# A second buffer for transposed blocks, paid for with shared places, in a graph attention and slice attention layer on one Trainium2 core

## The chip, the cores and the metric

The kernel runs on one core of one Trainium2 chip. The metric is the device time of one launch in microseconds (us). Before the change the median of three runs is 2681.41 us (2673.46 to 2681.55). The profiled execution has a span of 2673.3 us.

A core has a matrix engine (TensorE, PE in the profile, with its weight loads as PEld), a vector engine (VectorE, DVE), a scalar engine for functions such as Exp (ScalarE, ACT), GpSimd (POOL), and SyncE (SP), whose queue issues the DMA transfers here. All of them run at the same time, each through its own list of instructions in order, and wait for one another by semaphores.

## What is computed

The input x has 32 batches of 512 rows (nodes) and 256 features. Each batch passes two residual blocks. In short form:

```python
# block 1: graph attention, twice
o0 = relu(ln(x) @ mlp1_w + b1)                  # 512 x 512
h  = o0 @ W_fc                                  # unmasked attention
p  = softmax(leaky_relu(f1[i] + f2[j]), axis=j) # f1, f2: h times two vectors
o1 = elu(elu(p @ h)) + o0
o2 = relu(o1 @ mlp2_w + b2)                     # 512 x 256
h2 = o2 @ W_hand                                # attention masked by adj
p2 = softmax(where(adj > 0, leaky_relu(f1[i] + f2[j]), -9e15), axis=j)
x  = x + relu(elu(elu(p2 @ h2)) + o2)

# block 2: slice attention with 8 heads, 64 slices of 64 channels
xn = ln(x)
w  = softmax((xn @ W_x) @ W_slice / temperature)    # 512 x (8 x 64)
tokens = (w.T @ (xn @ W_fx)) / sum(w)               # per head
out_slice = softmax(q @ k.T / 8) @ v                # q, k, v from tokens
out = x + (w @ out_slice) @ W_out + b_out
```

Everything is in float32. The batches are independent of one another, and the kernel keeps up to four of them in progress.

## The kernel before

The kernel is written batch by batch and step by step, but isn't emitted in that order. A recorder takes down every operation with the tiles that it reads and writes; then a list scheduler with its own model of costs plays the program through, and the operations are emitted in the order of their modelled starts. TURNS gives each step of a batch a point in time that serves as its priority; HEAD and TAIL shift the steps of the first and the last three batches.

```python
TURNS = {
    "load": -145.1, "norm1": -102.2, "mlp1": 176.5, "h": 203.5, "factors": 206.6, "p": 209.3,
    "pv": 219.9, "o1": 240.0, "mlp2": 243.4, "h2": 273.9, "e": 274.6, "p2": 274.6,
    "pv2": 305.6, "norm2": 314.1, "w": 376.2, "sums": 378.3, "s1T": 396.3, "tokens": 446.2,
    "att": 472.7, "vo": 472.7, "gg": 472.7, "out": 483.8,
}
PERIOD, SPARE = 92.2, 0.00
```

A tile belongs to a tag, and a tag has so many places (bufs, one by default) in on-chip memory. A tile can only be begun when a place of its tag is free, and the scheduler also keeps a queue for each tag: whose turn it is to take the next place. For most tags that queue runs through all batches in order; for tags that begin with "stage" each batch has a queue of its own.

```python
class _Log:
    def __init__(self, ap, age):            # age: number of the batch
        ...
        self.queue = self.tag, age if self.psum or self.tag.startswith("stage") else 0
```

Large transposes of inner batches don't run on PE. VectorE transposes 32x32 blocks into a stage tile, four DMAs write the stage to a scratch tensor in DRAM, and a fifth reads it back with the blocks in their new places (the first and the last batch use PE transposes instead):

```python
def flip(src, dst):
    nc.vector.transpose(dst, src.rearrange("p (c i) -> p c i", i=Q))      # Q = 32

def gather(what, stage, dst):
    blocks, width = stage.shape[1:]
    scr = dram.tile([blocks, Q, P // Q, width], F32, name="scr", tag=f"scr_{what}", bufs=2)
    for a in range(P // Q):
        nc.sync.dma_start(scr[:, :, a, :].rearrange("c r j -> r c j"), stage[ts(a, Q), :, :])
    nc.sync.dma_start(dst, scr.rearrange("(k c) r a j -> (c r) k (a j)", c=P // Q))
```

Three of these stages, u_stage, e_stage and w_stage, are 8 KiB per partition and share the tag "stage" with one place. The smaller ones (for xn, o2, xn2 and s1) share another tag, "stage4", also with one place.

```python
# step pv: unmasked attention, for each block i of 128 rows
u, m = row("u"), row("m")                    # tags u and m, two places each
elu_elu([...], m, u)
flip(u, stage[:, :, ts(i, Q)])               # u_stage
# step o1
gather("u", stage, o1T)                      # then o1T += o0T on VectorE, four instructions

# step mlp2
o2T = new("o2T", [P, KD, N])
...  # 8 matmuls from o1T, two ScalarE instructions write o2T
# step e: masked attention, for each block i
...  # three VectorE instructions and one Exp on tile e
flip(e, stage[:, :, ts(i, Q)])               # e_stage
# step p2
gather("e", stage, pT)
...  # o2T is also transposed for the residual, through o2_stage
# step pv2
u, m = row("u2", (P, 2, D), "u"), row("m2", (P, 2, D), "m")
elu_elu(parts, m, u)

# step norm2
raw = new("xn2_raw", [P, KD, N], tag="raw4")
transpose_features("xn2", b, xn, raw, True)  # flips into xn2_stage, gather into raw
...  # two ScalarE copies from raw to xn2T
# step w
wt = softmax of (xn2T @ weff) by blocks of rows
flip(wt, stage_w[:, :, ts(t, Q)])            # w_stage
# step sums: s1 = w.T @ xn, gather("w", ...), four ScalarE copies into wT
# steps s1T, tokens
# steps att, vo
sc = new("sc2", [P, NP, G])
...  # softmax of the slice attention in sc, PE transposes of sc into pt
attT = new("attT", [P, NP, G])
nc.scalar.copy(attT, pt)
# steps gg, out
```

Of the kernel before, what the change touches and what calls it, by code (L numbers as in the profile page):

```python
# [13 lines left out]
ENGINES = ("tensor", "vector", "scalar", "gpsimd", "sync")  # L14

TURNS = {
    "load": -145.1, "norm1": -102.2, "mlp1": 176.5, "h": 203.5, "factors": 206.6, "p": 209.3,
    "pv": 219.9, "o1": 240.0, "mlp2": 243.4, "h2": 273.9, "e": 274.6, "p2": 274.6,
    "pv2": 305.6, "norm2": 314.1, "w": 376.2, "sums": 378.3, "s1T": 396.3, "tokens": 446.2,
    "att": 472.7, "vo": 472.7, "gg": 472.7, "out": 483.8,  # L20
}
PERIOD, SPARE = 92.2, 0.00

HEAD = (
    (-8, -8, 49, -10, -8, 25, 0, -39, -4, 6, -2, -2, -40, -2, -2, -2, -2, -2, 3, -8, 1, -20),
    (8, 2, 25, 1, 1, 0, 8, 8, 1, 1, -7, 0, 2, 2, 2, 2, 2, 2, 2, -5, 9, 2),
    (0, -1, -1, 0, 0, -22, 0, 12, 0, 1, 0, 0, 0, 0, 0, 0, 11, 0, 0, 0, -3, 0),
)
TAIL = (
    (0, 0, 53, 0, 0, 0, 0, 4, 0, 0, -6, 2, 0, 0, 0, 0, 2, 0, 3, 3, -5, 4),  # L30
    (0, 0, 17, 1, -2, -27, 0, -2, -4, -38, 0, 23, 1, -6, -2, 9, 2, 6, -2, -2, -2, -2),
    (-85, 1, 1, 1, 1, 16, 20, 22, 19, 19, 19, 7, 14, -7, 9, 9, -7, 0, -7, 0, -16, -30),
)


# [4 lines left out]
P = 128  # L40
# [4 lines left out]
class Recorder:  # L45
# [10 lines left out]
    def __init__(self, nc):  # L56
        self.nc, self.ops, self.logs, self.age, self.step = nc, [], {}, -1, ""
        self.joint = False
        for engine in ENGINES:
            setattr(self, engine, _Recording(self, engine))  # L60
# [215 lines left out]
class _Log:  # L276


    def __init__(self, ap, age):
        tensor = ap.tensor  # L280
        self.name, self.tag, self.bufs = tensor.name, tensor.tag, tensor.tag_meta.bufs
        self.psum = ap.space == bass.MemoryType.PSUM

        self.queue = self.tag, age if self.psum or self.tag.startswith("stage") else 0
        self.entries = []


# [22 lines left out]
def adj_ffn_kernel(  # L310
# [26 lines left out]
    B, N, D = x.shape  # L337
    HID = mlp1_w.shape[1]
    HH = HID // 2
    NT = N // P  # L340
    KD = D // P
    KH = HID // P
    HEADS = temperature.shape[1]
    G = W_slice.shape[1]
    C = W_slice.shape[0]
    INNER = HEADS * C
    NP = INNER // P
# [11 lines left out]
    def new(name, shape, bufs=1, tag=None, dtype=F32):  # L359
        return sbuf.tile(list(shape), dtype, name=name, tag=tag or name, bufs=bufs)  # L360

    def mm_tile(shape):
        return psum.tile(shape, F32, tag="mm", name="mm", bufs=5)
# [8 lines left out]
    Q = 32  # L372
# [5 lines left out]
    def by_dma(what, b):  # L378

        return what in FLIPPED and b not in EDGES  # L380
# [35 lines left out]
    def load_x(b):  # L416
# [14 lines left out]
        out=ident, in_=ident, compare_op=OP.not_equal, fill=1.0, base=0,  # L431
# [160 lines left out]
    for p in range(NP):  # L592
        pv = mm_tile([P, D])
# [49 lines left out]
    def front(b):  # L643
# [21 lines left out]
        h = new("h", [P, NT, 2, HH + 1])  # L665
# [49 lines left out]
        nc.step = "pv"  # L715
        o1T = new("o1T", [P, KH, N])
        if by_dma("u", b):
            stage = new("u_stage", [P, HID // Q, P], tag="stage")
        for i in range(NT):
            pms = [mm_tile([P, HH + 1]), mm_tile([P, HH])]  # L720
            for s, pm in enumerate(pms):
# [21 lines left out]
        if by_dma("u", b):  # L743
            gather("u", stage, o1T)
            for m in range(KH):
                o1 = o1T[:, m, :].rearrange("p (t a i) -> p t a i", t=NT, i=Q)
# [3 lines left out]
    def middle(b, o1T):  # L750

        nc.step = "mlp2"
        o2T = new("o2T", [P, KD, N])
        for m in range(KD):
            pm = mm_tile([P, N])
            for k in range(KH):
                nc.tensor.matmul(
                    pm.rearrange("p (a t i) -> p a t i", t=NT, i=Q), w2[:, k, ts(m)],
                    swapped(o1T[:, k, :]), start=(k == 0), stop=(k == KH - 1),
                )  # L760
            nc.scalar.activation(o2T[:, m, :], pm, AF.Relu, bias=b2[:, m : m + 1])
        nc.step = "h2"
        h = new("h2", [P, NT, D + 2])
        for t in range(NT):
            pm = mm_tile([P, D + 2])
            for k in range(KD):
                nc.tensor.matmul(
                    pm, o2T[:, k, ts(t)], wh[:, k, :], start=(k == 0), stop=(k == KD - 1)
                )
            nc.scalar.copy(h[:, t, :], pm)  # L770
        f2b = tr_tile([P, N])
        for j in range(NT):
            nc.tensor.transpose(f2b[:, ts(j)], h[:, j, D + 1 : D + 2].to_broadcast([P, P]), ident)
        if not by_dma("e", b):
            pt, f2b = f2b, new("f2b", [P, N], tag="acb")
            nc.scalar.copy(f2b, pt)
        nc.step = "e"
        pT = new("p2T", [P, NT, N])
        if by_dma("e", b):
            stage = new("e_stage", [P, N // Q, P], tag="stage")  # L780
        nmax = small("nmax", [P, NT])
        for i in range(NT):
            e = new("e", [P, N], bufs=2)
            nc.vector.scalar_tensor_tensor(
                e, f2b, h[:, i, D : D + 1], mbias[:, i, :], op0=OP.add, op1=OP.add
            )
            nc.vector.scalar_tensor_tensor(e, e, ALPHA, e, op0=OP.mult, op1=OP.max)
            nc.vector.tensor_reduce(
                nmax[:, i : i + 1], e, axis=AX.X, op=OP.max, negate=True
            )  # L790
            nc.scalar.activation(e, e, AF.Exp, bias=nmax[:, i : i + 1])
            if by_dma("e", b):
                flip(e, stage[:, :, ts(i, Q)])
                continue
            pt = tr_tile([P, NT, P])
            for j in range(NT):
                nc.tensor.transpose(pt[:, j, :], e[:, ts(j)], ident)
            nc.scalar.copy(
                pT.rearrange("p j (t a i) -> p j t a i", t=NT, i=Q)[:, :, :, i, :],
                pt.rearrange("p j (t i) -> p j t i", i=Q),  # L800
            )
        nc.step = "p2"
        if by_dma("e", b):
            gather("e", stage, pT)

        nc.vector.memset(h[:, :, D], 1.0)

        r2 = new("r2", [P, NT, D])
        stage = new("o2_stage", [P, N // Q, KD * Q], tag="stage4")
        for k in range(KD):  # L810
            nc.vector.transpose(
                stage[:, :, ts(k, Q)].rearrange("p (t a) i -> p t a i", t=NT),
                swapped(o2T[:, k, :]),
            )
        gather("o2", stage, r2)

        x1 = new("x1", [P, NT, D], bufs=2)
        nc.sync.dma_start(x1, x[b].rearrange("(p t) d -> p t d", p=P))
        nc.step = "pv2"
        for i2 in range(NT // 2):  # L820
            parts = []
            for s in range(2):
                i = 2 * i2 + s
                pm = mm_tile([P, D + 1])
                for j in range(NT):
                    nc.tensor.matmul(
                        pm, pT[:, j, ts(i)], h[:, j, : D + 1], start=(j == 0), stop=(j == NT - 1)
                    )
                rd = small("rd2", [P, 1])
                nc.vector.reciprocal(rd, pm[:, D : D + 1])  # L830
                parts.append((pm[:, :D], rd, s))
            u, m = row("u2", (P, 2, D), "u"), row("m2", (P, 2, D), "m")
            elu_elu(parts, m, u)
            for s in range(2):
                u3 = u[:, s, :].rearrange("p (k a i) -> p k a i", k=KD, i=Q)
                r3 = r2[:, 2 * i2 + s, :].rearrange("p (a k i) -> p k a i", k=KD, i=Q)
                nc.vector.tensor_tensor(u3, u3, r3, op=OP.add)
            nc.vector.scalar_tensor_tensor(
                x1[:, ts(i2, 2), :], u, 0.0, x1[:, ts(i2, 2), :], op0=OP.max, op1=OP.add
            )  # L840
        return x1

    def back(b, x1):
# [4 lines left out]
        layernorm(x1, xn, "ln2")  # L848
        xnT = new("xn2T", [P, KD, N])
        if by_dma("xn2", b):  # L850
            raw = new("xn2_raw", [P, KD, N], tag="raw4")
            transpose_features("xn2", b, xn, raw, True)
            for k in range(KD):
                nc.scalar.copy(
                    xnT[:, k, :].rearrange("p (t a i) -> p t a i", t=NT, i=Q), swapped(raw[:, k, :])
                )
        else:
            transpose_features("xn2", b, xn, xnT, False)

        nc.step = "w"  # L860
        w = new("w", [P, NT, INNER])
        wT = new("wT", [P, NP, N])
        if by_dma("w", b):
            stage_w = new("w_stage", [P, INNER // Q, P], tag="stage")
        for t in range(NT):
            pm = mm_tile([P, INNER])
            for k in range(KD):
# [29 lines left out]
        if by_dma("s1", b):  # L897
            stage = new("s1_stage", [P, D // Q, P], tag="stage4")
# [20 lines left out]
        if by_dma("w", b):  # L919
            raw = new("w_raw", [P, NP, N], tag="w")  # L920
# [6 lines left out]
        s1T = med("s1T", (P, KD, INNER))  # L927
# [74 lines left out]
        pt = tr_tile([P, NP, G])  # L1002
        for q in range(NP // 2):
            nc.tensor.transpose(pt[:, ts(q, 2), :], sc[:, ts(q, 2), :], ident)
        attT = new("attT", [P, NP, G])
        nc.scalar.copy(attT, pt)
        pa = mm_tile([P, NP, G])
        halves(pa, tokbd, attT)
# [2 lines left out]
        gg = med("gg")  # L1011
        for p2 in range(NP // 2):
            pg = mm_tile([P, 2, D])
            for s in range(2):
                p = 2 * p2 + s
# [87 lines left out]
```

## Time and profile before

| what | value |
|---|---|
| median of three runs | 2681.41 us (2673.46 to 2681.55) |
| span of the profiled execution | 2673.3 us |
| instructions | 35248 |
| DMA traffic | 375.40 MB, mean 140 GB/s |
| ACT busy | 1093.4 us (41%) |
| POOL busy | 111.8 us (4%) |

The page gives for every engine its busy time and its share of the span; then the span in 40 equal slices with the busy share of each in tenths (9 is 90% or more), and the clock that PE was granted, in tenths of full speed. As every operation is emitted by the same helper line of the kernel (L273), groups are told apart by the tiles they write and read: "mm<-h,pT" is a matmul into a tile mm from h and pT. "mm" is the tag of most matmul outputs, "tr" that of PE transposes. One float32 matmul shows as two records. In a list of waits, "PE mm <- DVE o1T" is time in which PE could not start a matmul because VectorE had not yet written o1T. In a timeline a bracket after a line gives the idle time of the engine just before it and what ended it.

### The profile page before, as it was taken

The page shows a single profiled execution, that of the slowest core. Times are in us where ns is not written, and L with a number is a line of the kernel's source. Part 1 is how long each engine was busy: PE and PEld are TensorE (multiplying, and loading weights), DVE is VectorE, ACT ScalarE, POOL GpSimd, SP SyncE. Part 2 cuts the span into 40 slices and gives each one's busy share as a digit, 9 for nine tenths or more (in the row PEclk, how much of TensorE's full clock was granted, in tenths as well). Part 3 has the DMA queues.
Part 4 walks back from the last instruction along what each step waited for, and adds up shares of the span by engine and source line. Part 5 has one row for each costly group of instructions (what it writes and reads, how often), then busy time and mean ns, then how long its engine had stood idle before and what let it go on. Part 6 is the DMA issues. An engine that isn't in the chain of part 4 may idle for free.

```text
span 2673.3 us, 35248 instructions
## 1 busy us (share of the span) xinstructions
PE 2608.7 (98%) x12477; PEld 1929.1 (72%) x12477; DVE 2081.2 (78%) x5161; ACT 1093.4 (41%) x2009; POOL 111.8 (4%) x171
## 2 busy tenths in 40 slices
PE   7999999999999999999999999999999999999997
PEld 5776667777777777777777777776777767777775
DVE  6577778877778877779877788777788777888785
ACT  3443344433444433444434444334444334444341
POOL 1000000000000000000000000000000000000000
PEclk9999999999999999999999999999999999999998
DMA  5125455554455454556554555544564545554440
GB/s 162 52 67 148 122 156 166 152 156 132 137 166 166 137 161 116 147 168 165 148 141 128 157 166 148 154 127 139 168 172 134 154 122 150 166 158 142 127 119 23
DMA packets 465657, 375.40 MB, mean 140 GB/s; under 512 B 86597, under 2 KB 382665, under 8 KB 465481
## 3 DMA queue, kind: packets, MB, share of 16 engines
q1 hardware_dynamic: 463896, 372.10, 49.6%
q8 instruction: 99, 1.62, 0.2%
q10 hardware_dynamic: 1584, 1.05, 0.1%
q14 instruction: 78, 0.63, 0.1%
HBM read 197.96 MB, written 175.11 MB: 140 GB/s over the span
## 4 chain that ended last, share of the span: by engine, by line
PE 45%; DVE 29%; DMA 16%; issue 3%; SPq 3%; POOL 2%; ACT 1%; DVEq 0%; ACTq 0%
PE mm L273 43%; DMA xt<-in_x_dram 5%; DVE u L273 4%; DVE e L273 3%; DMA o1T<-scr 3%; DMA scr<-e_stage 3%; SPq L273 3%; PE tr L273 2%; DVE w L273 2%; POOL ln_rstd L273 2%; DVE e_stage L273 2%; DVE w_stage L273 2%; DMA scr<-u_stage 2%; DVE m L273 1%; DVE u_stage L273 1%
## 5 line engine op out<-in xcount | busy, mean ns | idle before, releaser
L273 PE MATMUL mm<-wfc,o0T 128*128 128x257 f32 x2048 | 479.3, 381 | 0.0
L273 PE MATMUL mm<-h,pT 128*128 128x257 f32 (+1 forms) x2048 | 468.1, 380 | 4.2 <-DVE pT L273 4.2
L273 PEld LDWEIGHTS mm<-wfc,o0T 128*128 128x128 f32 x2048 | 381.9, 189 | 82.2 <-issue 24.8
L273 PEld LDWEIGHTS mm<-h,pT 128*128 128x128 f32 x2048 | 385.2, 190 | 64.3 <-DVE pT L273 6.7
L273 ACT COPY h<-mm 128x257 f32<-128x257 f32 (+1 forms) x384 | 142.9, 372 | 302.2 <-PE mm L273 295.8
L273 PE MATMUL mm<-xn,w 128*128 128x257 f32 x1024 | 255.1, 383 | 4.0 <-ACT w L273 3.3
L273 PE MATMUL mm<-xnT,w 128*128 128x512 f32 x512 | 240.4, 600 | 10.8 <-DMA xnT<-scr 7.3
L273 PE MATMUL mm<-gg,wT 128*128 128x256 f32 x1024 | 245.3, 379 | 0.0
L273 PE MATMUL mm<-h,p2T 128*128 128x257 f32 x1024 | 244.9, 380 | 0.3 <-ACT o0T L273 0.3
L273 PE MATMUL mm<-o1T,w 128*128 128x512 f32 x512 | 227.4, 596 | 13.4 <-DVE o1T L273 10.8
L273 PE MATMUL mm<-weff,xn2T 128*128 128x512 f32 x512 | 231.7, 595 | 0.0
L273 PEld LDWEIGHTS mm<-h,p2T 128*128 128x128 f32 x1024 | 191.4, 190 | 31.3 <-ACT o0T L273 0.7
L273 PEld LDWEIGHTS mm<-xn,w 128*128 128x128 f32 x1024 | 187.8, 191 | 35.0 <-issue 8.9
L273 PEld LDWEIGHTS mm<-gg,wT 128*128 128x128 f32 x1024 | 191.7, 190 | 28.6 <-issue 1.0
L273 PEld LDWEIGHTS mm<-o1T,w 128*128 128x128 f32 x512 | 94.8, 190 | 131.0 <-issue 94.5
L273 DVE STREAM_TRANSPOSE o_stage<-o2T 128x512 f32<-128x512 f32 x64 | 45.5, 710 | 163.6 <-ACT o2T L273 163.6
L273 ACT ACTIVATE e<-e,nmax 128x512 f32<-128x512 f32 x128 | 92.4, 722 | 186.0 <-DVE nmax L273 184.5
L273 DVE SCALAR_TENSOR_TENSOR e<-tr,h,mbias 128x512 f32<-128x512 f32 x120 | 86.6, 742 | 99.3 <-PE tr L273 99.3
L273 ACT ACTIVATE m<-m 128x512 f32<-128x512 f32 x192 | 120.9, 630 | 102.4 <-DVE m L273 102.1
L273 PEld LDWEIGHTS mm<-weff,xn2T 128*128 128x128 f32 x512 | 93.0, 191 | 92.3 <-issue 90.5
L273 PEld LDWEIGHTS mm<-xnT,w 128*128 128x128 f32 x512 | 92.2, 191 | 93.1 <-issue 72.7
L273 ACT ACTIVATE w<-w 128x512 f32<-128x512 f32 x128 | 80.7, 631 | 177.2 <-DVE w L273 177.0
(151 smaller groups left out, 3798.9 us busy)
## 6 DMA issues: line engine op xcount, KB each, us to landing
scr<-xn_stage SPq DMA_DIRECT2D x240, 128.0 KB, 2.5
scr<-u_stage SPq DMA_DIRECT2D x120, 256.0 KB, 4.1
o1T<-scr SPq DMA_DIRECT2D x30, 1024.0 KB, 6.0
scr<-e_stage SPq DMA_DIRECT2D x120, 256.0 KB, 3.8
p2T<-scr SPq DMA_DIRECT2D x30, 1024.0 KB, 5.5
scr<-w_stage SPq DMA_DIRECT2D x120, 256.0 KB, 4.6
w_raw<-scr SPq DMA_DIRECT2D x30, 1024.0 KB, 7.3
x<-in_x_dram SPq DMA_DIRECT2D x32, 512.0 KB, 5.7
```

What stands on the lines that cost most here:

```text
L273: getattr(getattr(self.nc, op.engine), op.method)(*op.args, **op.kwargs)
```

## The change

The change gives the tag "stage" a second place, so that the blocks of two of the three large transposes can be held at once. That takes 8 KiB more per partition. Room for it comes from two tiles that lose places of their own: xn2_raw (4 KiB) moves into the place of o2T, and attT (1 KiB) into that of sc2. In the scheduler, the row tiles u and m, which the two graph attentions of a batch both use, get a queue per batch, as the stages have: a batch's unmasked attention may then take a row before an earlier batch's masked attention has taken its own. Tags carry a suffix after the name, so "u_" and "m_" stand for the tags u and m alone. All the turns and the shifts of the first and last three batches are new. What is computed, and with which instructions, doesn't change; their order on each engine does.

```diff
 TURNS = {
-    "load": -145.1, "norm1": -102.2, "mlp1": 176.5, "h": 203.5, "factors": 206.6, "p": 209.3,
-    "pv": 219.9, "o1": 240.0, "mlp2": 243.4, "h2": 273.9, "e": 274.6, "p2": 274.6,
-    "pv2": 305.6, "norm2": 314.1, "w": 376.2, "sums": 378.3, "s1T": 396.3, "tokens": 446.2,
-    "att": 472.7, "vo": 472.7, "gg": 472.7, "out": 483.8,
+    "load": -122.2, "norm1": 78.3, "mlp1": 267.5, "h": 296.1, "factors": 313.0, "p": 323.7,
+    "pv": 324.8, "o1": 324.8, "mlp2": 340.5, "h2": 360.8, "e": 385.5, "p2": 385.7,
+    "pv2": 430.7, "norm2": 437.4, "w": 494.8, "sums": 496.8, "s1T": 507.4, "tokens": 549.1,
+    "att": 558.0, "vo": 558.2, "gg": 560.3, "out": 593.0,
 }
-PERIOD, SPARE = 92.2, 0.00
+PERIOD, SPARE = 91.1, 0.01
# HEAD and TAIL: three rows of 22 shifts each, all new (cut)
@@ class _Log
-        self.queue = self.tag, age if self.psum or self.tag.startswith("stage") else 0
+        self.queue = self.tag, age if self.psum or self.tag.startswith(("stage", "u_", "m_")) else 0
@@ step pv
-            stage = new("u_stage", [P, HID // Q, P], tag="stage")
+            stage = new("u_stage", [P, HID // Q, P], bufs=2, tag="stage")
@@ step e
-            stage = new("e_stage", [P, N // Q, P], tag="stage")
+            stage = new("e_stage", [P, N // Q, P], bufs=2, tag="stage")
@@ step norm2
-            raw = new("xn2_raw", [P, KD, N], tag="raw4")
+            raw = new("xn2_raw", [P, KD, N], tag="o2T")
@@ step w
-            stage_w = new("w_stage", [P, INNER // Q, P], tag="stage")
+            stage_w = new("w_stage", [P, INNER // Q, P], bufs=2, tag="stage")
@@ step vo
-        attT = new("attT", [P, NP, G])
+        attT = new("attT", [P, NP, G], tag="sc2")
```

## The prediction

> **What bounds the kernel now.** I read the busy table first, then the slices.
>
> ```profile
> PE 2608.7 (98%) x12477; PEld 1929.1 (72%) x12477; DVE 2081.2 (78%) x5161; ACT 1093.4 (41%) x2009; POOL 111.8 (4%) x171
> ...
> PE   7999999999999999999999999999999999999997
> ...
> PEclk9999999999999999999999999999999999999998
> ```
>
> TensorE (PE) is busy for 2608.7 of 2673.3 us, so all the gaps the profile shows on it come to 64.6 us. VectorE (DVE) is next at 78%. The third line, the granted clock, is full except at the very end. The next question is where those 64.6 us lie. The table by stretches, asked for four windows of 492 us (six batches each) and for the ends, answers:
>
> ```profile
> 500.00:992.00 492.00, 486.55 (x2328) 359.88 (x2327) 393.87 (x980) 206.25 (x378) 21.42 (x31) 1.00 0.54 150
> 992.00:1484.00 492.00, 487.44 (x2330) 360.72 (x2330) 395.15 (x981) 205.94 (x377) 21.31 (x30) 1.00 0.54 151
> ...
> 0.00:50.00 50.00, 34.79 (x147) 25.99 (x148) 29.29 (x102) 14.30 (x28) 6.55 (x18) 0.94 0.67 195
> ...
> 2600.00:2640.00 40.00, 34.17 (x185) 24.12 (x184) 27.78 (x63) 12.91 (x24) 1.26 (x2) 0.83 0.17 55
> 2640.00:2674.00 34.00, 22.39 (x153) 17.48 (x151) 10.24 (x29) 3.55 (x8) 0.00 (x0) 0.87 0.05 17
> ```
>
> After the length of the stretch come the busy times of PE, PEld, DVE, ACT and POOL, then clock, DMA share and GB/s. In the middle PE misses 492 - 486.55 = 5.45 us and 4.56 us per six batches, under 1 us a batch. The first 50 us miss 15.2 us, and the last 74 us miss 5.8 + 11.6 = 17.4 us, at a clock of 0.83 to 0.87 as well. So three places could give time: start, middle and end.
>
> The middle's waits of PE, in the window from 500 to 2400 us:
>
> ```profile
> PE mm L273 <- DVE o1T L273: 9.3, 12, 1.3
> PE mm L273 <- DMA xnT<-scr: 7.0, 14, 1.0
> PE mm L273 <- DVE tok L273: 1.6, 9, 0.2
> ```
>
> The numbers are us in total, times, and the longest one. All PE waits of this window come to 22.0 us, and these three are 17.9 of it. None names a transposed-block buffer; mlp2 waits for o1T and mlp1 for xnT, one after the gather through DRAM and an add on DVE, the other after its gather alone. The timeline shows where they recur (1417.56 and 1499.08 us are the same step of two successive batches, as are other starts 24 periods apart, 443.49 and 2393.48 us, which give 1949.99 / 24 = 81.25 us a batch).
>
> ```profile
> 1417.56 1.10 PE L273 MATMUL mm<-xnT,w 128*128 128x512 f32 x2 [0.61 <-DMA xnT<-scr]
> ...
> 1435.06 7.11 PE L273 MATMUL mm<-o1T,w 128*128 128x512 f32 x16 [0.35 <-PE mm L273]
> ```
>
> **What the skill says.** The Trainium skill, "Perfetto Trace Analysis", section "Identifying the Most-Contended Engine", says that matmul busy share is no good measure of the distance to the peak, because pipelined matmuls overlap, and asks for the weight-load share instead. The trace agrees: 16 records of 512 columns start over 7 us (1435.06 to 1442.00), one per 0.43 us, while each is shown as about 0.6 us. So gaps under some 0.17 us are hidden in "busy", and PEld is at 72%, not 98%. Its section "Optimization Strategy" says that a gap repeating on the saturated engine can mean too little SBUF or PSUM for the next tile. The gap repeats here, but its releasers are the chains' ends, so the trace gives this only indirect support. "TensorE: Matmul & The Clock Gate", section "HAM oscillation", says that gaps over about 3.4 us lower the clock. The one gap of that size near the end (4.40 us, for s1T at 2608.39 us) lies in the stretch with clock 0.83, which agrees. "SBUF — State Buffer", section "SBUF size: 192, 224, or 256?", gives about 208 KiB per partition as usable; no run so far shows the limit, but it explains why room must be freed.
>
> **The change, part by part.** No arithmetic, no matmul and no transfer is added or removed: the same 2608.7 us of PE work stay, give or take overlap. Everything acts through order and waiting.
>
> 1. *Second stage buffer* (8 KiB more). From the DVE and DMA timelines of one batch: u_stage is held from its first flip at 1414.28 us to the landing of its four writes, issued until 1424.4 and landing some 4.1 us later, 14 us; e_stage from 1451.30 to 1467.1 us, 16 us; w_stage from 1467.86 us to about 1481 us, 13 us. One buffer is thus held 43 of 81.25 us. The hand-over is tight in one place:
>
> ```profile
> 1462.34 4.74 DMA scr<-e_stage
> ...
> 1467.94 1.81 DVE w_stage L273 x3
> ```
>
> This is the chain of waits: the first flip of w comes 0.8 us after the writes from e_stage landed at 1467.1. That row of w was finished at 1461.7 us, so the flip waited about 6 us. But DVE did other work meanwhile, and the copies into wT end near 1412 us in one batch while the out matmuls that read them start at 1461: about 49 us of slack. So the removed 6 us lie off the path of PE. Direct gain: near 0. What it buys is freedom in the order.
>
> 2. *Rows u and m free of the batches' order.* Before, the unmasked attention of batch b+1 could take a row only after the masked attention of batch b had taken its two. The PE timeline shows the two interleaved matmul by matmul around 1400 us. Freed, pv may run ahead of pv2 by up to that stage's 16 x 0.434 = 6.9 us, and u_stage, gather and o1T follow earlier. That is more than the largest o1T wait (1.3 us). I expect most of the 9.3 us to go, and a part of the 7.0 us of xnT, since the new turns also put load and norm1 apart. I take 60% of the 16.3 us: 9.8 us over 1900 us; scaled to some 2200 us of full pipeline, **11 us**.
>
> 3. *xn2_raw in o2T's place* (4 KiB back). Now o2T of batch b+1 can't be written before xn2_raw of batch b has been copied out. The ACT timeline of before shows how near that is:
>
> ```profile
> 1435.51 1.14 ACT L273 COPY xn2T<-xn_raw 128x512 f32<-128x512 f32 x2 [0.83 <-DMA xn_raw<-scr]
> 1438.77 0.69 ACT L273 ACTIVATE o2T<-mm,b 128x512 f32<-128x512 f32 x1 [2.12 <-PE mm L273]
> ```
>
> The copies end at 1436.65 us, 2.1 us ahead of the write. The order fits already, but it becomes a loop: from an o2T write to the end of the copies of the same batch takes 1436.65 + 81.25 - 1438.77 = 79.1 us of an 81.25 us period. I charge **2 us** over the run for batches in which 2.1 us is not enough.
>
> 4. *attT in sc2's place* (1 KiB back). attT is copied at 1427.74 us from a transpose that has already read sc. It waited for that anyway: 0.
>
> 5. *New turns, head and tail.* The start holds 21.5 us of gaps up to 300 us, of which 8.4 us (the first xn) and 4.0 us (the first pT) are the first batch's own latency, which no order removes. The end holds 17.4 us, and the reduced clock costs about 40 x 0.17 + 34 x 0.13 = 11 us more, if lost time follows the clock. The last batch's chain (tokens, attention, vo) has nothing left beside it, so I expect only a small share of these 50 us: **6 us**.
>
> Sum: -11 + 2 - 6 = -15 us. As the starting point I take 2677 us, between the lowest and the highest of the three runs (2673.46 and 2681.55). That gives **2662 us**, 0.7% under the median of 2681.41.
>
> **Rivals.** *(a) Nothing moves.* PE is at its limit and the second buffer removes only waits that are hidden. For it: part 1 has no PE wait beside it. Against it: the o1T wait exists and its chain starts with the rows. Time: 2673 to 2681. *(b) The loop of part 3 becomes the bound.* The new turns spread a batch over 715 us instead of 629, and later masked attention means later norm2 and a later xn2_raw. If the loop exceeded the period by 1 us, each of about 28 batches would lose 1 us: 2690 to 2705. For it: the slack of only 2.1 us and DVE at 78%. Against it: the order is worked out with this constraint inside. *(c) The ends gain a lot.* If half the 50 us of head and tail came back: 2640. For it: both tables are wholly new and larger. Against it: they only shift turns, and the end is a chain of dependent steps. *(d) More reordering means more switching between streams on PE* and more short waits, hidden in "busy": PE busy would rise with the same work, up to 10 us.
>
> **Range and chances.** A 2% gain means below 2627.8 us, 49 us off the starting point: most of the shown gaps, or all of the middle's and half of the ends'. I give it 0.04. A 2% loss means above 2735, nearly 2 us more in every batch, which only rival (b) in a strong form makes: 0.03. The range from (c) to a mild (b) is 2636 to 2690.
>
> **What would show it.** Right: PE busy near 2600 to 2610, the middle's PE waits near 12 us instead of 22, o1T nearly gone from them, a period near 80.8 us; the flips of w no longer follow the landing of e_stage. Part 3 is wrong if ACT's o2T write is released by the copies of xn2_raw, or PE waits for o2T grow. Part 5 is wrong if the last 74 us miss much less than 17 us of PE. The total is wrong if PE busy itself changes by over 20 us, which no step of mine foresees.

## The result, and the profile after

The changed kernel takes 2647.49 us (median; 2645.28 to 2651.99) against 2679.29 us for the kernel before in the same measurement: a ratio of 0.9887, with a 95% interval of 0.9865 to 0.9909. That is 32 us less, where 19 us less than the median of before had been predicted.

The busy times of the page of after:

```profile
PE 2602.6 (98%) x12477; PEld 1930.1 (73%) x12477; DVE 2094.5 (79%) x5161; ACT 1082.1 (41%) x2009; POOL 92.0 (3%) x171
```

The span fell from 2673.3 to 2645.1 us, 28.2 us, and PE's gaps from 64.6 to 2645.1 - 2602.6 = 42.5 us, which is 22.1 us of it. The other 6.1 us left the busy time, although the instructions are as many; that fits short waits hidden in overlapping records, but no view shows it. The table by stretches of after, in the columns of the one before, says where:

```profile
0.00:50.00 50.00, 35.88 (x149) 26.94 (x150) 29.27 (x102) 14.40 (x28) 6.55 (x18) 0.95 0.65 195
...
500.00:992.00 492.00, 489.57 (x2343) 363.24 (x2342) 399.90 (x987) 204.38 (x380) 16.68 (x31) 1.00 0.53 152
992.00:1484.00 492.00, 490.19 (x2373) 362.78 (x2372) 400.46 (x985) 207.70 (x387) 16.49 (x30) 1.00 0.52 150
...
2571.00:2611.00 40.00, 34.34 (x192) 25.13 (x191) 26.73 (x63) 11.31 (x21) 1.26 (x2) 0.87 0.14 46
2611.00:2645.20 34.20, 24.28 (x161) 19.08 (x158) 11.97 (x33) 5.11 (x11) 0.00 (x0) 0.85 0.08 32
```

The two stretches of the middle miss 2.4 and 1.8 us instead of 5.5 and 4.6. The last 74 us miss 15.6 us instead of 17.4, at the same low clock. Summed over the whole trace, PE's gaps before and after are 23.0 and 15.0 us up to 500 us, 23.3 and 9.9 us from there to 2468 us, and 18.3 and 17.5 us in the rest. So of the gaps 8.0 us came from the start, 13.4 from the middle and 0.8 from the end. The period of the middle went from 81.30 to 80.47 us a batch (starts of mlp2, 21 periods).

The middle's waits of PE, again from 500 to 2400 us, are complete in four lines and come to 9.6 us instead of 22.0:

```profile
PE mm L276 <- DVE pT L276: 3.8, 21, 0.2
PE mm L276 <- DVE o1T L276: 3.7, 6, 1.2
PE mm L276 <- DVE w L276: 1.3, 1, 1.3
PE mm L276 <- DVE tok L276: 0.8, 1, 0.8
```

The wait for xnT is gone and that for o1T is down from 9.3 to 3.7 us. PE's timeline shows what stands there now:

```profile
1456.65 2.77 PE L276 MATMUL mm<-h,p2T 128*128 128x257 f32 x12
1459.26 1.03 PE L276 MATMUL mm<-h,pT 128*128 128x257 f32 x4
...
1462.85 11.85 PE L276 MATMUL mm<-h,pT 128*128 128x256 f32 x54
1474.53 3.64 PE L276 MATMUL mm<-h,p2T 128*128 128x257 f32 x16
1478.10 1.15 PE L276 MATMUL mm<-s1T,wfx 128*64 128x64 f32 x32
...
1479.62 2.84 PE L276 MATMUL mm<-xnT,w 128*128 128x512 f32 x6
```

The second half of an older batch's masked attention (16 records on p2T, 3.64 us) comes after the younger batch's unmasked attention (pT). In the kernel before both halves of p2T were done some 12 us before pT ended, and mlp1 followed s1T with a wait for xnT. Now those 3.64 us are PE work that stands before mlp1. The order is only possible with the freed rows: its pT blocks take rows u and m while the older batch still has its second pair of rows to take.

What the second stage is used for is seen on DVE's timeline:

```profile
1439.07 0.70 DVE L276 STREAM_TRANSPOSE e_stage<-e 128x512 f32<-128x512 f32 x1
1445.10 0.70 DVE L276 STREAM_TRANSPOSE w_stage<-w 128x512 f32<-128x512 f32 x1
...
1455.05 0.70 DVE L276 STREAM_TRANSPOSE w_stage<-w 128x512 f32<-128x512 f32 x1
```

The gather of e, which waits for its writes, was issued at 1446.37 us; the first flip of w came 1.3 us earlier, so two stages overlap by little. But the four flips of w are now spread over 10 us, each after its row is done, where before three of them stood in one block once the stage came free.

### The profile page after: what moved, and what is told of

Its sections match the earlier page's. It is cut to its first block, busy times and chain, and to the rows that moved or that the text cites. A ratio compares the mean times of both kernels' runs of the same rounds, so it can differ in the third digit from the quotient of the medians.

```text
span 2645.1 us, 35403 instructions
## 1 busy us (share of the span) xinstructions
PE 2602.6 (98%) x12477; PEld 1930.1 (73%) x12477; DVE 2094.5 (79%) x5161; ACT 1082.1 (41%) x2009; POOL 92.0 (3%) x171
## 4 chain that ended last, share of the span: by engine, by line
PE 79%; DVE 11%; DMA 5%; ACT 3%; issue 1%; SPq 1%; POOL 0%; DVEq 0%; ACTq 0%
PE mm L276 76%; PE tr L276 3%; DVE pT L276 2%; DMA o1T<-scr 2%; DMA w_raw<-scr 2%; DMA scr<-u_stage 1%; DVE s L276 1%; DVE s_stage L276 1%; ACT m L276 1%; ACT acb L276 1%; DVE acb L276 1%; DVE w_stage L276 1%; DVE u L276 1%; SPq L276 1%; DVE ln_st L276 1%
## 5 line engine op out<-in xcount | busy, mean ns | idle before, releaser
L276 PE MATMUL mm<-wfc,o0T 128*128 128x257 f32 x2048 | 494.4, 381 | 0.0
L276 PE MATMUL mm<-h,pT 128*128 128x256 f32 (+1 forms) x2048 | 467.2, 382 | 8.5 <-DVE pT L276 8.4
L276 PE MATMUL mm<-xn,w 128*128 128x257 f32 x1024 | 249.4, 380 | 1.3 <-DVE w L276 1.3
L276 ACT ACTIVATE u<-mm,rd 128x256 f32<-128x256 f32 x192 | 89.7, 467 | 269.8 <-PE mm L276 151.0
L276 DVE SCALAR_TENSOR_TENSOR u<-m,u 128x512 f32<-128x512 f32 x192 | 129.7, 686 | 32.7 <-ACT m L276 30.9
```

Of the source, the lines that this page charges most:

```text
L276: getattr(getattr(self.nc, op.engine), op.method)(*op.args, **op.kwargs)
```

## The experiments

All were timed in up to five rounds against the kernel before; a ratio is to that kernel, with its 95% interval.

**The new turns alone**: the kernel before, with the changed TURNS, PERIOD, SPARE, HEAD and TAIL and none of the other edits.

> The kernel before with only the new turns, period, head and tail shifts; one stage buffer, rows in the order of the batches, own places for xn2_raw and attT. Theory A (places and rows are what gives the gain, the new turns only use them): at most a third of the 32 us comes, 2665 to 2690 us, and the middle's waits of PE for o1T and xnT stay near 16 us. Theory B (the turns alone carry it, the buffers and rows are beside the point): 2645 to 2655 us.

3929.41 us, ratio 1.4664 (1.4641 to 1.4687). Both theories were far off. From the page, the busy times and the clock by slices:

```profile
PE 2957.0 (75%) x12477; PEld 2065.3 (53%) x12477; DVE 2169.5 (55%) x5161; ACT 1078.9 (27%) x2009; POOL 89.7 (2%) x171
...
PEclk9988898888998888988889888889888899888778
```

and the first line of PE's waits over the whole run:

```profile
PE mm L276 <- DMA s1T<-scr: 358.5, 29, 16.0
```

A batch now takes 120 us. The turns and the queue contradict each other. In the new turns a younger batch's pv (324.8 + 91.1 = 415.9) comes before the older one's pv2 (430.7); in the old ones it came after it (219.9 + 92.2 = 312.1 against 305.6), and the queue of rows demands that. PE waits some 12 us a batch for s1T; that nothing else is at hand then because of this contradiction is the likely reading, and the run of rows in order below, with the same contradiction, breaks down alike.

**Places and rows alone**: all edits except turns and tables.

> The kernel before with the second stage buffer, the shared places and the freed rows, but with all the old turns and shifts. Theory A (freed rows let the unmasked attention run ahead by itself): 2655 to 2670 us with a smaller o1T wait. Theory B (turns carry it): within 5 us of before, 2672 to 2685 us.

2782.46 us, ratio 1.0386 (1.0372 to 1.04), period 85.1 us. Neither theory again: the old turns lose 100 us when the places and queues that they were made for are changed. Turns and structure are a pair.

**The changed kernel, one stage again.**

```diff
-            stage = new("u_stage", [P, HID // Q, P], bufs=2, tag="stage")
+            stage = new("u_stage", [P, HID // Q, P], tag="stage")
# the same for e_stage and w_stage
```

> The changed kernel with one stage buffer again; freed rows, shared places and new turns kept. My step 1 (second buffer removes only hidden waits): within 5 us of the changed kernel, 2643 to 2653 us. Rival (the new turns need two stages at once, e and w or w and u overlapping): 2660 to 2700 us, with waits of PE for o1T or wT.

2703.4 us, ratio 1.0091 (1.0077 to 1.0105), period 81.56 us: the rival's range, though not by the waits it named. In the middle PE waits 4.5 us for o1T (3.7 in the changed kernel) and never for wT.

**The changed kernel, rows in order again.**

```diff
-        self.queue = self.tag, age if self.psum or self.tag.startswith(("stage", "u_", "m_")) else 0
+        self.queue = self.tag, age if self.psum or self.tag.startswith("stage") else 0
```

> The changed kernel with rows u and m given out in the order of the batches again; two stages, shared places and new turns kept. My step 2 (the freed rows are what takes away the waits before mlp2 and mlp1): most of the gain is lost, 2662 to 2680 us, the o1T wait back near 9 us in the middle. Rival (rows don't matter): within 5 us of the changed kernel, 2643 to 2653 us.

4028.87 us, ratio 1.5037 (1.5017 to 1.5058), period 123 us: the same breakdown as with the turns alone. For these turns the freed rows are a condition, not an addition.

**How much hangs on the exact order**: one constant of the changed kernel.

```diff
-PERIOD, SPARE = 91.1, 0.01
+PERIOD, SPARE = 91.3, 0.01
```

> The changed kernel with the constant PERIOD at 91.3 instead of 91.1, which has no meaning of its own and only shifts priorities. If the gain belongs to the structure and is robust: 2645 to 2655 us. If it hangs on the exact order that was found: the period leaves 80.5 us by several us, 2700 us or more; then what an undone part cost under unchanged turns says little about that part.

2782.1 us, ratio 1.0368 (1.0348 to 1.0388), period 84.65 us: a loss of 135 us by a constant with no meaning of its own. So the 56 us of the one-stage run can't be read as the worth of the second stage. A fair comparison needs turns made for each structure.

**Turns searched anew for four structures.** For each I searched TURNS and PERIOD at random with the scheduler's own model, with about the same effort, and left HEAD and TAIL empty. For two stages with rows in order the short search gave nothing usable, and the long one began from the old turns. "One, freed" and both two-stage versions have the shared places, so what the sharing alone costs is not separated.

```diff
-TURNS = {"load": -122.2, "norm1": 78.3, ...}
+TURNS = {...}          # found for the structure of each run
-HEAD = ((6, -12, ...), ...)
-TAIL = ((-3, 1, ...), ...)
+HEAD = ()
+TAIL = ()
```

> The structure of before (one stage, rows in order, own places) with turns that I searched anew for it and with empty head and tail tables. Theory B2 (the gain is effort in the search of turns, any structure would give it): a period of 80.5 us or less and within 5 us of the changed kernel without shifts. Theory A2 (the structure allows an order that the old one does not): the period stays at 81.0 us or more, the total at least 10 us above the changed kernel without shifts.

> Freed rows and shared places, but one stage buffer, with turns searched anew for this structure and empty head and tail tables. If the second buffer matters by itself: a period of 81.0 us or more as in the changed kernel cut back to one stage (81.55). If it does not (my step 1) and its loss there was a matter of turns made for two: a period near 80.5 us, total within 10 us of the changed kernel without shifts.

> Two stages and shared places, but rows in the order of the batches, turns searched anew for this structure, empty head and tail tables. If both the second stage and the freed rows are needed together: no better than the searched old structure, a period of 82 us or more, 2700 us or more. If the second stage alone gave the gain: a period near 80.5 us and 2650 to 2665 us.

> The changed structure (two stages, shared places, freed rows) with turns searched anew in the same way as for the other two, and empty head and tail tables. If structure counts, this is the fastest of the three searched ones, 10 us or more below the old structure, and near the changed kernel without shifts or a little below, 2640 to 2665 us. If only the search counts, the three agree within 5 us.

| stages, rows | median us | ratio to before (95%) | period us | PE waits, 500 to 2400 us | PE's share of the chain |
|---|---|---|---|---|---|
| one, in order | 2709.82 | 1.0106 (1.0092 to 1.0119) | 82.2 | 32.7 | 34% |
| two, in order | 2708.56 | 1.0099 (1.0074 to 1.0124) | 82.0 | 33.1 | 54% |
| one, freed | 2693.24 | 1.0043 (1.0027 to 1.0059) | 81.9 | 23.7 | 55% |
| two, freed | 2649.93 | 0.9884 (0.9871 to 0.9898) | 80.0 | 3.8 | 88% |

The last column is from the page. The chain is followed back from the last instruction, at each step to what released it or to the instruction before it on its engine, and the share is what PE has of it. One of the five launches of "one, freed" took 4572.12 us at a mean clock of 0.556 and is left out of its ratio.

With both edits the search ends 60 us below the old structure; with the second stage alone it gains 1 us. The 17 us of "one, freed" must not be read as the worth of the freed rows, for its order makes no use of them in the middle. PE's timeline shows a batch's masked attention complete before the next one's unmasked attention begins, as the old queue demands:

```profile
1396.05 7.19 PE L265 MATMUL mm<-h,p2T 128*128 128x257 f32 x32
1403.08 7.29 PE L265 MATMUL mm<-h,pT 128*128 128x257 f32 x32
```

That holds from the third batch on in all three slower versions, while in "two, freed" half of the 32 records on p2T follow the first one on pT. So the 17 us rather show how far apart two searches can end, and what stands clear of them are the 43 us between "two, freed" and the best of the other three. Structure counts (theory B2 falls), and only with both edits did a search find the order with pv ahead and its period of 80.0 us. The waits of PE in the middle with one stage and freed rows:

```profile
PE mm L265 <- DVE o1T L265: 12.9, 14, 1.7
PE mm L265 <- DVE w L265: 7.9, 21, 0.6
```

and DVE in the same kernel and window:

```profile
DVE o1T L265 <- DMA o1T<-scr: 50.3, 23, 3.3
DVE w_stage L265 <- DMA scr<-e_stage: 7.3, 16, 1.0
```

Here DVE does stand still for the place: its first flip of w is held until the writes from e_stage have landed. With both edits no such line is left, and PE's longest waits are these:

```profile
PE mm L265 <- DVE o1T L265: 1.5, 4, 0.6
PE mm L265 <- DMA xnT<-scr: 1.5, 4, 0.6
```

In that kernel the first flip of w comes between the second and the third flip of e, so two stages are in use for longer than in the changed kernel.

A search at random isn't a proof of the best order for a structure, and each was made once. For the old structure it was not the best: the turns of the kernel before reach a period of 81.5 us without tables and 81.3 us with them, against 82.2 us from the search, though the totals without tables are close (2712.68 and 2709.82 us). So the 60 us are too many as the worth of the two edits. The fairer figure sets the best known version of each structure side by side, both with tables: 38 us, in the last run below. For one edit alone there is no such second version.

**What head and tail tables are worth.** Both kernels with both tables emptied.

> The changed kernel with empty head and tail tables; places, rows and turns as changed. My step 5 (head and tail are worth about 6 us of the change): 2652 to 2658 us. Rival (the ends carry a large part): 2662 to 2675 us, the period of the middle still 80.5 us.

> The kernel before with empty head and tail tables. The changed kernel's tables were worth about 12 us. If the old ones were worth less, the difference is what the new tables add to the change: at 2690 us they add 2 us, at 2685 us 7 us; my step 5 said 6. If the old ones were worth as much or more (2692 us or over), the ends add nothing.

The changed kernel without tables takes 2660.98 us, ratio 0.9927 (0.9913 to 0.9941); the kernel before without tables 2712.68 us, ratio 1.0114 (1.0094 to 1.0133). So the new tables are worth 13 us (2660.98 - 2647.49, from two measurements; 11 us by the ratios), the old ones 30 us (2712.68 - 2682.34). Without tables the change is worth 52 us; the tables take some 17 to 20 of it back, mostly because the new order has a better start by itself. Up to 500 us PE is busy for 457.0 us in the old order without tables and 477.0 us with them, in the new one for 478.9 and 485.0 us.

**A better version.** The searched turns for the full structure, with tables searched in the same way.

> The changed structure with the newly searched turns (2650 us without shifts) and head and tail tables searched for them. If the ends can be shortened as in the changed kernel, by some 8 us: 2638 to 2646 us, just under the changed kernel. If these ends are already at their chain of dependent steps: 2646 to 2652 us.

2644.32 us, ratio 0.9858 (0.9839 to 0.9877), period 79.97 us. It beats the kernel before by 38 us. Against the changed kernel it is 3 us lower in another measurement, with overlapping intervals: not told apart.

## Why the prediction was right, and which steps were not

The time lies in the range, in its better half, and the bound was named rightly: PE's work stayed and only its waiting could be won. But the gain was twice the 15 us of the sum, and the better half of the range was there for rival (c), a large gain at the ends. The time fell there because of the middle, which is in part luck. The term of the sum that was mis-sized is the middle: 11 - 2 = 9 us were predicted, while the period fell by 0.83 us, about 20 us over the 24 batches between 500 and 2468 us (an estimate from the two periods).

**Step 1, the second stage, failed.** It said "direct gain: near 0", because it followed the late flips of w only to the readers of wT, with 49 us of slack, and put the removed 6 us off the path of PE. The chain of before, as the profile infers it, says otherwise. From the landing of e_stage and the flips of w that step 1 shows, it goes on through DVE's work in order to the next load of xt, and by norm1 and its gather to a wait of mlp1 for xnT, one of the waits that the prediction lists (start, length and link of the chain, in order of time):

```profile
1475.12 6.00 DMA xt<-in_x_dram
...
1494.62 4.33 DMA xnT<-scr
...
1499.08 1.10 PE mm L273 x2
```

A list of waits names only the last link, xnT. Over the whole run scr<-e_stage holds 3% of the chain before and none of it after, and PE's own share grew. The two lines are the chain by engine, before and after:

```profile
PE 45%; DVE 29%; DMA 16%; issue 3%; SPq 3%; POOL 2%; ACT 1%; DVEq 0%; ACTq 0%
PE 79%; DVE 11%; DMA 5%; ACT 3%; issue 1%; SPq 1%; POOL 0%; DVEq 0%; ACTq 0%
```

Still the second stage alone gave 1 us in the searched orders, so this link isn't the only one that holds the order. With freed rows the searches differ by 43 us (2693.24 - 2649.93). I had written that the stage buys freedom in the order, and then put no price on that.

**Step 2, the rows, had a mechanism that the trace confirms in part, and too small a size.** The waits for o1T and xnT fell from 16.3 to 3.7 us, 12.6 us in the window instead of the 9.8 assumed. The pv step does pass pv2, as the timeline shows. The wait for xnT went another way than predicted: the second half of pv2 now fills the time before mlp1. And I took the rows as one gain among five; they are the condition for these turns (4028.87 us without them), and with one stage the search made no use of them.

**Step 3, the loop over o2T's place**, was charged 2 us. ACT's timeline of after:

```profile
1418.34 1.14 ACT L276 COPY xn2T<-xn_raw 128x512 f32<-128x512 f32 x2 [5.21 <-DMA xn_raw<-scr]
1419.51 0.69 ACT L276 ACTIVATE o2T<-mm,b 128x512 f32<-128x512 f32 x1
```

The o2T write now follows the copies directly; the 2.1 us of slack are used up, which I had named as the sign of a cost. Yet PE's list of waits in the middle has no line for o2T, so PE lost nothing visible; what it would gain with a place of its own for xn2_raw wasn't tried. **Step 4** (attT, 0) shows no wait of PE in the middle either.

**Step 5, the ends, was near in size (6 us predicted, 8.0 from the start and 0.8 from the end), but the tables did not bring it:** the new ones are worth less than the old ones. The start is better by the new order itself: without tables it already has PE busier up to 500 us (478.9 us) than the old order with tables (477.0 us).

**The rivals.** (a) falls: the middle gained. (b), a period set by the o2T loop, didn't come, though the period of the two breakdowns shows how much a wrong pairing of turns and queues can cost; I hadn't listed that. (c) falls too: it needs half of the ends' 50 us, and 8.8 us came back. (d) goes the other way: PE's busy time fell by 6 us.

## What to carry to other kernels

A list of waits names the last link only, so follow the chain further back before you call a wait for a place harmless: here the stage stood several links before PE's wait for xnT. Where the order of instructions is fixed ahead, judge a buffer or a freed queue by the orders that it allows, and look in the trace whether an order makes use of it at all. Don't undo one part under the old tuning and call the loss its worth: a constant with no meaning of its own cost 135 us here. Tune each version alike first, and more than once, for two searches that left the order of the rows the same in the middle ended 17 us apart.

## What the runs showed of the hardware

Waits on PE can cost more than their length. With the turns alone PE's busy time was 2957.0 us for the same 12477 records that take 2602.6 us in the changed kernel, and the mean granted clock was 0.87 instead of 0.995. One wait of that run on PE's timeline:

```profile
1433.71 1.97 PE L276 MATMUL mm<-s1T,wfx 128*64 128x64 f32 x32 [12.67 <-DMA s1T<-scr]
```

and the stretch just after it in the table by stretches, with the clock third from the end:

```profile
1433.70:1456.00 22.30, 15.84 (x95) 10.99 (x96) 4.83 (x11) 1.89 (x5) 0.00 (x0) 0.50 0.31 86
```

The clock stays at 0.50 for 22 us after the wait, and the 32 records take 1.97 us instead of the 1.15 us of the changed kernel. At half the clock some 8 of the 15.84 busy us are lost; over 30 such batches that would be about 240 of the 354 us by which the busy time grew, an estimate from this one stretch. The rest is not assigned.

The wait of 12.67 us fits the Trainium skill, "TensorE: Matmul & The Clock Gate", section "HAM oscillation", which puts the limit at gaps of about 3.4 us. But shorter gaps were followed by a lower clock too. In the run with PERIOD at 91.3 the longest gap in the 8 us before this drop is 1.34 us; the first line is from PE's timeline, the second from the table by stretches:

```profile
762.46 4.09 PE L276 MATMUL mm<-xn,w 128*128 128x257 f32 x10 [1.34 <-DVE w L276]
...
763.00:766.40 3.40, 3.40 (x10) 2.56 (x9) 3.40 (x10) 0.58 (x1) 0.00 (x0) 0.50 0.37 143
```

In the kernel before, too, the clock is 0.50 from 245.2 to 248.6 us after a gap of 2.39 us. So 3.4 us of idling is not a safe limit here, and the one gap of 4.40 us that the prediction found in agreement doesn't prove it. In the middle of the changed kernel, with no gap over 1.3 us, the clock stays at 1.00; what exactly lowers it the runs don't show.
